# Graph convolution on one core: later program places for the stores of gathered rows, 88 early tiles for 92, and a node stage on fixed PSUM banks

## The chip, the cores and the metric

The kernel runs on one core of a Trainium2 chip. The metric is the device time of one execution in microseconds (us), the median of several runs; lower is better. The five engines appear in the profile as PE (TensorE matmul, with PEld its weight loads), DVE (VectorE), ACT (ScalarE), POOL (GpSimd) and SP (SyncE, here only a DMA queue).

## The reference, cut to what matters

There are N = 12500 nodes with 160 values each (64 scalars, 32 vectors of 3) and 400000 edges, sorted by destination.

```python
h = jnp.maximum(_layernorm(x, axis=-1), 0.0)
s0, y0 = x0 @ W_sc0 * a, x0 @ W_l1_0 * a        # x0, x1: the parts of h; a: node_vec1
...                                             # s1, y1: the same of x1, a row for each component
w = jax.nn.silu(edge_length_embedded @ fc_W1) @ fc_W2          # 192 weights for each edge
ys0, ys1 = y0[edge_src], y1[edge_src]                          # the gather
mid = products of w, ys and the 4 values of edge_attr          # 96 + 96*3 = 384 for each edge
z = zeros.at[edge_dst].add(mid)                                # the scatter
x = x + (C_S * s + C_X * (z @ W_l2) * a)
```

(Scales are left out, and the last four lines are put in short.) So each node is normalized and mapped once to y and s, each edge takes the row y of its source, and the products are summed by destination.

## The kernel before, in words

Nodes stand in 98 tiles of 128 rows, edges in 3125 tiles of 128, four edge tiles to a block (782 blocks), twelve to a group.

**The node stage** (the loop over q, L424 to L439) takes two node tiles a step and eight a group, in 49 steps. It is a software pipeline: in iteration q each stage function handles step q minus its lag. `center` (DVE, lag 0) makes mean and variance and one tile's rows; `center_second` (ACT, lag 1) the other tile's; `turn_rows` (TensorE, lag 2) transposes them into a PSUM tile pt; `out_of_psum` (ACT L380, lag 3) copies pt to hT; `map_rows` (TensorE L388, L389, lag 4) multiplies hT with the weights into PSUM tiles po; `leave` (ACT L399, lag 5) copies po, scaled, to ys, and at the end of a group stores eight tiles of y to the DRAM tensor y_d with a DMA on ACT's queue (L401); `add_s` (DVE L407, lag 6) adds the self connection to acc. These y_d stores are called by their group, 0 to 12; the last group has two tiles, the others eight.

**The edge stage** (the loop over b) runs for each block: `load` issues four gathers of y rows on POOL (L509, `yg<-y_d,src_sb`; each takes the 128 rows that one edge tile names), eight blocks ahead, into nine buffers; TensorE makes the edge weights (L519, L535); DVE the products (L458 to L470) and the one-hot matrix sel (L552); TensorE sums by destination (L572). The first gather of y_d needs every y_d store to have landed.

**Early rows.** Every 32nd block, 23 of them (`RB`, capped by the number of blocks), doesn't gather y. Its 4 tiles gather rows of x instead, which are there from the start. `gather_x` (L326, `xr<-in_x,src_sb`) issues these 92 gathers on POOL in the node stage, the first half at q = 4, the second at q = 16, into twelve buffers, and stores each four tiles to a DRAM tensor xr_d with one DMA on SP's queue (L329). In the edge stage `made_load` (L644) brings them back as xm, and the functions `made_...` normalize, transpose and map them on DVE, TensorE and ACT, in steps that `plan` spreads over the blocks before.

**What sets the order.** PE, ACT and DVE run their instructions in the order written (`manual_schedule`). SP and POOL don't: when the program is built, the framework lists their instructions by its own estimate of times, and place in the program is a priority. Each queue then runs its list in order. Every direct DMA, on SP's queue or ACT's, also takes one of eight completion counters in turn, in the order of the common list, and is issued only when the DMA before it on the same counter has landed. So each waits for the one eight places before it in the list, whichever queue that is on.

On SP the program writes, in this order: the loads of x, src and dst; at q = 4 the stores of xr_d number 0 to 10, then 23 small weight loads (L218 to L231), one load of edge attributes (raw, L263) and the first block's eight xe loads (L255); at q = 16 the stores 11 to 22; after the loop the edge stage's loads, with the next eight xe loads first. In the list of before, the y_d store of group 2 stands after the third xr_d store, that of group 3 after six weight loads, that of group 4 after the last weight load, that of group 5 after store 12, that of group 6 after store 21, and that of group 7 after the next xe and raw loads. Groups 8 to 12 follow with no SP DMA between them.

On POOL the node stage also has a `partition_all_reduce` (L139), which turns the destinations' minima around, and a few memsets.

Of the kernel before, what the change touches and what calls it, by code (L numbers as in the profile page):

```python
# [10 lines left out]
F32 = mybir.dt.float32  # L11
# [4 lines left out]
PSUM = bass.MemoryType.PSUM  # L16
DRAM = bass.MemoryType.DRAM

P = 128
M0 = 64  # L20
M1 = 32
D = M0 + 3 * M1
# [8 lines left out]
EG = 8  # L31
GN = 8
HN = 2
RB = 24
RS = 32
LO = D - P
EPS = 1e-5
# [5 lines left out]
def kernel(  # L43
# [19 lines left out]
    nc = tc.nc  # L63
# [19 lines left out]

    nr = max(0, min(RB, (NB - 1) // RS - 1))
    RT = nr * GT
    xr_d = dram.tile([max(nr, 1) * P, GT * D], F32, name="xr_d")
# [193 lines left out]
    def by_tile(ap):  # L280
        n = ap.shape[0]
        return ap.rearrange("(t p) c -> p t c", p=min(P, n))
# [9 lines left out]
    with (  # L292
        tc.tile_pool(name="nr", bufs=1) as nrp,
        tc.tile_pool(name="nrx", bufs=12) as nrx,
        tc.tile_pool(name="ny", bufs=2) as ny,
        tc.tile_pool(name="ns", bufs=3) as ns,
        tc.tile_pool(name="nh", bufs=4) as nh,
        tc.tile_pool(name="nd", bufs=3) as nd,
        tc.tile_pool(name="nd_pt", bufs=2, space=PSUM) as nd_pt,
        tc.tile_pool(name="nd_po", bufs=6, space=PSUM) as nd_po,  # L300
    ):
        yss, mvs, ras, hs, lesses, pts, hTs, poss = ({} for _ in range(8))
        steps = [(g, n, j, min(HN, n - j)) for g, n in groups for j in range(0, n, HN)]

        def load_x(g, n):
            if g + n == NT and N % P:
                nc.gpsimd.memset(acc[:, NT - 1, :], 0.0)
            node_dma(g, n, lambda rows, t, p: nc.sync.dma_start(acc[:p, g + t.start:g + t.stop, :],
                                                                by_tile(x[rows, :])))

        def find_x():

            of = src_sb[:, RS * GT:RS * GT * (nr + 1)].rearrange("p (r c) -> p r c", c=RS * GT)[:, :, 0:GT]
            whole = nrp.tile([P, nr, GT], I32, name="whole")
            nc.vector.tensor_scalar(whole, of, 7, None, ALU.arith_shift_right)
            nc.vector.tensor_copy(hi_f.rearrange("p (r c) -> p r c", c=GT), whole)
            nc.vector.tensor_copy(lo_f.rearrange("p (r c) -> p r c", c=GT), of)
            nc.vector.scalar_tensor_tensor(lo_f, hi_f, -float(P), lo_f, op0=ALU.mult, op1=ALU.add)

        def gather_x(lo, hi):  # L320

            for r in range(lo, hi):
                xr = nrx.tile([P, GT, D], F32, name="xr")
                for k in range(GT):
                    c = (r + 1) * RS * GT + k
                    nc.gpsimd.indirect_dma_start(  # L326
                        out=xr[:, k, :], out_offset=None, in_=x,
                        in_offset=bass.IndirectOffsetOnAxis(ap=src_sb[:, c:c + 1], axis=0))
                nc.sync.dma_start(xr_d[r * P:(r + 1) * P, :], xr.rearrange("p t c -> p (t c)"))  # L329

        def center(q):

            g, n, j, m = steps[q]
            xt = acc[:, g:g + n, :]
            if j == 0:
                mvs[g] = ns.tile([P, GN, 2], F32, name="mv")
            mv = mvs[g]
            h = nh.tile([P, HN, D], F32, name="h")
            for k in range(m):
                st = ns.tile([P, 6], F32, name="st")  # L340
                nc.vector.bn_stats(st, xt[:, j + k, :])
                nc.vector.bn_aggr(mv[:, j + k, :], st)
                if k == 0:
                    nc.vector.tensor_scalar(h[:, k, :], xt[:, j + k, :], mv[:, j + k, 0:1], 0.0, ALU.subtract, ALU.max)
                else:
                    less = ns.tile([P, 1], F32, name="less")
                    nc.vector.tensor_scalar(less, mv[:, j + k, 0:1], -1.0, None, ALU.mult)
                    lesses[q] = less
            hs[q] = h
            if j + m == n:  # L350
                ra = ns.tile([P, GN], F32, name="ra")
                nc.scalar.activation(ra[:, :n], mv[:, :n, 1], AF.Sqrt, bias=eps)
                ras[g] = ra

        def center_second(q):

            g, n, j, m = steps[q]
            if m > 1:
                nc.scalar.activation(hs[q][:, 1, :], acc[:, g + j + 1, :], AF.Relu, bias=lesses.pop(q))

        def scales(q):

            g, n, j, m = steps[q]
            if j + m == n:
                ra = ras[g]
                nc.vector.reciprocal(ra[:, :n], ra[:, :n])
                nc.vector.tensor_mul(ra[:, :n], ra[:, :n], a_sb[:, g:g + n])

        def turn_rows(q):
            m, h = steps[q][3], hs.pop(q)  # L370
            pt = nd_pt.tile([P, 2, HN, P], F32, name="pt")
            for k in range(m):
                nc.tensor.transpose(pt[:, 0, k, :], h[:, k, 0:P], ident)
                nc.tensor.transpose(pt[:, 1, k, :], h[:, k, LO:D], ident)
            pts[q] = pt

        def out_of_psum(q):
            m, pt = steps[q][3], pts.pop(q)
            hT = nd.tile([P, 2, HN, P], F32, name="hT")
            nc.scalar.activation(hT[:, :, :m, :], pt[:, :, :m, :], AF.Copy)  # L380
            hTs[q] = hT

        def map_rows(q):
            m, hT = steps[q][3], hTs.pop(q)
            poss[q] = []
            for k in range(m):
                po = nd_po.tile([P, 2, D], F32, name="po")
                nc.tensor.matmul(po[:, :, 0:M0], hT[:, 0, k, :], wn0, start=True, stop=True)  # L388
                nc.tensor.matmul(po[:, :, M0:], hT[:, 1, k, :], wn1, start=True, stop=True)  # L389
                poss[q].append(po)  # L390

        def leave(q):

            g, n, j, m = steps[q]
            if j == 0:
                yss[g] = ny.tile([P, GN, 2, D], F32, name="ys")
            ys, ra = yss[g], ras[g]
            for k, po in enumerate(poss.pop(q)):
                nc.scalar.activation(ys[:, j + k, :, :], po, AF.Copy, scale=ra[:, j + k:j + k + 1])  # L399
            if j + m == n:  # L400
                node_dma(g, n, lambda rows, t, p: nc.scalar.dma_start(by_tile(y_d[rows, :]), ys[:p, t, 0, :]))  # L401

        def add_s(q):

            g, n, j, m = steps[q]
            if j + m == n:
                nc.vector.tensor_add(acc[:, g:g + n, :], acc[:, g:g + n, :], yss[g][:, :n, 1, :])  # L407


        with tc.manual_schedule(engines=engines):  # L410
            load_x(0, HN)
            nc.sync.dma_start(a_sb, attr)
            node_weights()
            load_x(HN, min(GN, NT) - HN) if NT > HN else None
            nc.sync.dma_start(src_sb, src)
            for k, (g, n) in enumerate(groups[1:]):
                load_x(g, n)
                if k == 4:
                    nc.sync.dma_start(dst_i, dst)
            if len(groups) <= 5:  # L420
                nc.sync.dma_start(dst_i, dst)
            last = len(steps) - 1
            half = nr // 2
            for q in range(len(steps) + 6):  # L424
                if q == min(4, last):
                    if RT:
                        find_x()
                        gather_x(0, half)
                    edge_weight_loads()
                    e4_load(0)  # L430
                    load_xe(0)
                if q == min(16, last):
                    first_nodes()
                    if RT:
                        gather_x(half, nr)
                for stage, lag in ((scales, 1), (center_second, 1), (leave, 5), (out_of_psum, 3), (turn_rows, 2), (map_rows, 4),
                                   (center, 0), (add_s, 6)):
                    if 0 <= q - lag <= last:
                        stage(q - lag)  # L439
    with tc.manual_schedule(engines=engines):  # L440
        edge_weights()
    before.close()
# [31 lines left out]
    with (  # L474
# [258 lines left out]
        with order:  # L733
# [17 lines left out]
            for b in range(K * (NG - 1) + 12):  # L751
                g, k = divmod(b, K)
# [3 lines left out]
                if b < NB:  # L756
                    q, r = divmod(b, EG * K)
# [36 lines left out]
    with (  # L794
# [11 lines left out]
        with tc.For_i(0, n, 1) as _:  # L806
# [60 lines left out]
            with tc.For_i(0, NT, 1) as i:  # L867
                zt = fp.tile([P, ZC], F32, name="f_zt")
                nc.sync.dma_start(zt, z_d[ds(i * P, P), :])
                pt = fpp.tile([P, 3, P], F32, name="f_pt")  # L870
# [4 lines left out]
                po = fpp.tile([P, D], F32, name="f_po")  # L875
# [50 lines left out]
```

## Time and profile before

| | us |
|---|---|
| median of 3 runs | 4006.47 (4003.85 to 4008.27) |
| the profiled execution | 4014.25 |
| its span | 4012.4 |
| PE busy | 3864.0 (96%) |
| DVE busy | 3519.4 (88%) |
| ACT busy | 2027.8 (51%) |
| POOL busy | 2979.7 (74%) |

The busy shares are means over both stages. A row of a timeline gives start, duration (both in us), engine, line, operation, tiles, count, and in brackets the idle time of the engine just before and what ended it. A row of the stretches gives for PE, PEld, DVE, ACT and POOL the busy time and the number of instructions, then the granted TensorE clock, the DMA share and GB/s. A row of the waits gives the total, the number of times and the longest. A row of the groups gives busy time, mean ns of one, and the idle time before. SPq and ACTq are the DMA issues of these queues; they are not counted as busy.

### The profile page before, as it was taken

The page shows a single profiled execution, that of the slowest core. Times are in us where ns is not written, and L with a number is a line of the kernel's source. Part 1 is how long each engine was busy: PE and PEld are TensorE (multiplying, and loading weights), DVE is VectorE, ACT ScalarE, POOL GpSimd, SP SyncE. Part 2 cuts the span into 40 slices and gives each one's busy share as a digit, 9 for nine tenths or more (in the row PEclk, how much of TensorE's full clock was granted, in tenths as well). Part 3 has the DMA queues.
Part 4 walks back from the last instruction along what each step waited for, and adds up shares of the span by engine and source line. Part 5 has one row for each costly group of instructions (what it writes and reads, how often), then busy time and mean ns, then how long its engine had stood idle before and what let it go on. Part 6 is the DMA issues. An engine that isn't in the chain of part 4 may idle for free.

```text
span 4012.4 us, 60400 instructions
## 1 busy us (share of the span) xinstructions
PE 3864.0 (96%) x18093; PEld 2382.8 (59%) x18093; DVE 3519.4 (88%) x7697; ACT 2027.8 (51%) x6160; POOL 2979.7 (74%) x3137
## 2 busy tenths in 40 slices
PE   5599999999999999999999999999999999999998
PEld 4455666665666656665666656656566566666655
DVE  6589899898899898898998998998998989989987
ACT  5455555555455544555454554555545554445444
POOL 6477777777777777777777777777777777777775
PEclk8799999999999999999999999999999999999999
DMA  8423333333233233232333323332332323342323
GB/s 254 119 74 79 74 79 77 76 76 78 75 78 79 73 79 77 74 79 73 80 77 76 78 76 76 77 79 73 79 79 74 78 74 79 77 126 75 74 74 83
DMA packets 239795, 334.86 MB, mean 83 GB/s; under 512 B 66506, under 2 KB 183318, under 8 KB 239206
## 3 DMA queue, kind: packets, MB, share of 16 engines
q0 software_dynamic: 150000, 256.20, 25.7%
q1 hardware_dynamic: 75666, 66.32, 5.6%
q10 hardware_dynamic: 13796, 8.44, 0.8%
q8 instruction: 144, 2.36, 0.2%
q14 instruction: 189, 1.55, 0.1%
HBM read 307.16 MB, written 23.54 MB: 82 GB/s over the span
## 4 chain that ended last, share of the span: by engine, by line
PE 69%; DVE 11%; POOL 7%; issue 5%; DMA 5%; ACT 1%; DVEq 1%; SPq 0%; ACTq 0%; POOLq 0%
PE pz L572 40%; PE pw L535 12%; PE px L519 8%; POOL yg L509 5%; DMA yg<-y_d,src_sb 5%; PE px L604 3%; DVE sel L552 3%; PE px L600 3%; POOL xr L326 2%; DVE tmp L460 2%; DVE tmp L458 2%; PE px L586 2%; DVE both L464 1%; DVE pr L470 1%; DVE pr L469 1%
## 5 line engine op out<-in xcount | busy, mean ns | idle before, releaser
L509 POOL DMA_INDIRECT yg<-y_d,src_sb x3033 | 2881.6, 950 | 966.7 <-issue 738.3
L572 PE MATMUL pz<-pr,sel 128*128 128x384 f32 x6250 | 2236.4, 501 | 22.4 <-DVE sel L552 22.3
L572 PEld LDWEIGHTS pz<-pr,sel 128*128 128x128 f32 x6250 | 1128.3, 190 | 827.6 <-issue 152.0
L453 ACT ACTIVATE yge<-yg,raw 128x160 f32<-128x160 f32 x3033 | 1133.0, 428 | 552.5 <-DMA yg<-y_d,src_sb 548.7
L536 ACT ACTIVATE pw<-raw 128x12 f32<-128x12 f32 x782 | 141.9, 181 | 1309.0 <-issue 664.9
L535 PE MATMUL pw<-w,hT 64*128 64x192 f32 x6250 | 722.3, 350 | 26.3 <-DVE pr L470 24.2
L466 DVE TENSOR_TENSOR pr<-both,pw 128x768 f32<-128x768 f32 x782 | 737.7, 943 | 0.0
L458 DVE TENSOR_TENSOR tmp<-yg,pw 128x384 f32<-128x384 f32 x759 | 417.5, 550 | 347.4 <-DMA yg<-y_d,src_sb 275.8
L535 PEld LDWEIGHTS pw<-w,hT 64*128 64x128 f32 x6250 | 491.5, 186 | 334.6 <-issue 92.3
L460 DVE TENSOR_REDUCE tmp<-tmp 128x128 f32<-128x384 f32 x782 | 464.4, 594 | 26.9
L552 DVE TENSOR_TENSOR sel<-pz,drel 128x1536 f32<-128x1536 f32 (+1 forms) x261 | 455.1, 1744 | 0.0
L519 PE MATMUL px<-xe,w 32*128 32x512 f32 x782 | 438.9, 643 | 4.9 <-issue 4.3
L470 DVE TENSOR_TENSOR pr<-pw,yge 128x384 f32<-128x384 f32 x782 | 427.6, 547 | 0.0
L469 DVE TENSOR_TENSOR pr<-pw,yge 128x256 f32<-128x256 f32 x782 | 326.3, 417 | 1.7 <-ACT yge L453 1.7
L464 DVE TENSOR_TENSOR both<-pw,yg 128x256 f32<-128x256 f32 x759 | 314.2, 414 | 0.0
L524 ACT ACTIVATE hT<-px 128x512 f32<-128x512 f32 x391 | 232.7, 595 | 3.0 <-PE px L519 2.8
L465 DVE TENSOR_TENSOR pr<-pw,tmp 128x128 f32<-128x128 f32 x782 | 219.3, 280 | 0.0
L600 PEld LDWEIGHTS px<-os,place 128*128 128x128 f32 x1044 | 169.8, 190 | 69.9 <-ACT ps L615 0.8
L604 PE MATMUL px<-wc,za 128*128 128x96 f32 (+1 forms) x1566 | 210.0, 270 | 0.0
L630 DVE SCALAR_TENSOR_TENSOR acc<-ps,a_sb,acc 128x160 f32 x522 | 198.8, 381 | 11.8 <-ACT ps L615 2.3
L604 PEld LDWEIGHTS px<-wc,za 128*128 128x128 f32 x1566 | 201.7, 191 | 0.5 <-ACT za L590 0.3
L600 PE MATMUL px<-os,place 128*128 128x160 f32 x1044 | 184.7, 299 | 1.1 <-ACT os L610 0.6
(119 smaller groups left out, 2238.8 us busy)
## 6 DMA issues: line engine op xcount, KB each, us to landing
yg<-y_d,src_sb POOLq DMA_INDIRECT x3033
xe<-in_e SPq DMA_DIRECT2D x784, 32.0 KB
y_d<-ys ACTq DMA_DIRECT2D x12, 640.0 KB
xr_d<-xr SPq DMA_DIRECT2D x23, 320.0 KB
xm<-xr_d SPq DMA_DIRECT2D x23, 320.0 KB
acc<-in_x SPq DMA_DIRECT2D x11, 640.0 KB
out<-acc SPq DMA_DIRECT2D x11, 640.0 KB
raw<-in_e SPq DMA_DIRECT2D x32, 192.0 KB
```

The costliest lines, as they stand in the source:

```text
L453: nc.scalar.activation(yge[:, k, :], yg[:, k, :], AF.Copy, scale=e4v[:, k, 0:1])
L458: nc.vector.tensor_tensor(tmp[:, :n, 0:3, :], y1, wt[:, :n, NW:NW + 3].unsqueeze(3).to_broadcast([P, n, 3, M1]), ALU.mult)
L460: nc.vector.tensor_reduce(tmp[:, :n, 3, :], tmp[:, :n, 0:3, :].rearrange("p t c u -> p t u c"), AX.X, ALU.add)
L466: nc.vector.tensor_mul(pr[:, :n, 192:ZC].rearrange("p t (c u) -> p t c u", c=3), both[:, :n, :].unsqueeze(2).to_broadcast([P, n, 3, M0]), ...
L470: nc.vector.tensor_mul(pr[:, :n, 96:192].rearrange("p t (c u) -> p t c u", c=3), wt[:, :n, M0:96].unsqueeze(2).to_broadcast([P, n, 3, M1]) ...
L509: nc.gpsimd.indirect_dma_start(out=yg[:, k, :], out_offset=None, in_=y_d, in_offset=bass.IndirectOffsetOnAxis(ap=src_sb[:, t:t + 1], axis=0))
L519: nc.tensor.matmul(ph, w1[r, :], xe[r, :], start=True, stop=True)
L535: nc.tensor.matmul(pw[:, k, 0:NW], hT[r, o:o + P], w2[r, :], start=True, stop=True)
L552: nc.vector.tensor_tensor(sels[g][:, 0:n, :], pzs[g % 2][:, ZC:].unsqueeze(1).to_broadcast([P, n, WN]), drel[:, g * TG:g * TG + n].unsquee ...
L572: nc.tensor.matmul(z_ps[g], sels[g][:, t % TG, :], pr[:, k, :], start=t % TG == 0, stop=last)
L600: nc.tensor.matmul(px[:, 1 + h, :], place[:, h, :], os[:, :], start=True, stop=True)
L604: nc.tensor.matmul(px[:, 0, lo:hi], za[:, k, :], wc[:, k, lo:hi], start=k == 0, stop=k == 1)
```

## The change

Four things change.

1. `RB` goes from 24 to 22. With 782 blocks it was capped at 23, so 22 blocks and 88 tiles are early now, in place of 23 and 92. The 23rd block gathers y like the rest.
2. `gather_x` no longer stores. The stores go to `keep_x`, which the loop over q calls at its end for store r as soon as 5q is at least 14r + 60 (r = 0 at q = 12, then every 2.8 steps); stores 16 to 21 follow after the loop.
3. The PSUM tiles of the node stage are eight fixed banks, two for pt and six for po, in place of tiles from two pools of the same sizes.
4. In each iteration `out_of_psum` comes before `leave`, the lag of `leave` is 6 (it was 5) and that of `add_s` 7 (it was 6), and the loop has one iteration more. ACT's wait for pt in one iteration so covers the po tiles that it reads next.

```diff
-RB = 24
+RB = 22
...
-        tc.tile_pool(name="nd_pt", bufs=2, space=PSUM) as nd_pt,
-        tc.tile_pool(name="nd_po", bufs=6, space=PSUM) as nd_po,
+        tc.tile_pool(name="nd_banks", bufs=1, space=PSUM) as nd_banks,
     ):
+        pt_banks = [nd_banks.tile([P, 2, HN, P], F32, name=f"pt{i}") for i in range(2)]
+        po_banks = [nd_banks.tile([P, 512], F32, name=f"po{i}") for i in range(6)]
...
+        xrs, kept = {}, [0]
...
-                nc.sync.dma_start(xr_d[r * P:(r + 1) * P, :], xr.rearrange("p t c -> p (t c)"))
+                xrs[r] = xr
+
+        def keep_x(r):
+            nc.sync.dma_start(xr_d[r * P:(r + 1) * P, :], xrs.pop(r).rearrange("p t c -> p (t c)"))
...
-            pt = nd_pt.tile([P, 2, HN, P], F32, name="pt")
+            pt = pt_banks[q % 2]
...
-                po = nd_po.tile([P, 2, D], F32, name="po")
+                po = po_banks[(q * HN + k) % 6][:, 0:2 * D].rearrange("p (v c) -> p v c", v=2)
...
-            for q in range(len(steps) + 6):
+            for q in range(len(steps) + 7):
...
-                for stage, lag in ((scales, 1), (center_second, 1), (leave, 5), (out_of_psum, 3), (turn_rows, 2), (map_rows, 4),
-                                   (center, 0), (add_s, 6)):
+                for stage, lag in ((scales, 1), (center_second, 1), (out_of_psum, 3), (leave, 6), (turn_rows, 2), (map_rows, 4),
+                                   (center, 0), (add_s, 7)):
                     if 0 <= q - lag <= last:
                         stage(q - lag)
+                while kept[0] in xrs and 5 * q >= 14 * kept[0] + 60:
+                    keep_x(kept[0])
+                    kept[0] += 1
+            while kept[0] in xrs:
+                keep_x(kept[0])
+                kept[0] += 1
```

## The prediction

> **What bounds the kernel now.** I read the page's head first, then POOL's waits, then the timeline of each queue in the first 200 us, and the stretches last.
>
> ```profile
> span 4012.4 us, 60400 instructions
> ```
> ```profile
> POOL yg L509 <- issue: 738.3, 2422, 0.3
> POOL yg L509 <- ACT yge L453: 46.9, 154, 0.3
> ...
> POOL yg L509 <- DMA y_d<-ys: 42.4, 1, 42.4
> ```
> ```profile
> 183.23 0.95 POOL L509 DMA_INDIRECT yg<-y_d,src_sb  x1 [42.40 <-DMA y_d<-ys]
> ...
> 3988.18 0.95 POOL L509 DMA_INDIRECT yg<-y_d,src_sb  x1 [0.31 <-issue]
> ```
> ```profile
> 120.00:140.00 20.00, 0.00 (x0) 0.00 (x0) 0.00 (x0) 0.00 (x0) 15.12 (x17) 0.50 0.46 131
> ...
> 3000.00:3500.00 500.00, 494.87 (x2304) 302.47 (x2303) 451.80 (x974) 256.94 (x785) 378.36 (x400) 1.00 0.30 77
> ```
>
> TensorE is busy 494.87 of 500 us in the edge stage, and yet it is not what sets the end. The waits of POOL say so: its third figure is the longest single wait, and every one of its waits but one is 0.3 us, the gap between two gathers. POOL is never held back by a full buffer. It issues 3033 gathers without a pause, the first at 183.23 and the last at 3988.18, which makes (3988.18 - 183.23) / 3032 = 1.255 us a gather. After the last one's end (3989.13) come 23.3 us of drain. So
>
> span = T0 + gathers x 1.255 + 23.3, with T0 = 183.23, the end of POOL's one long wait, for the last y_d store.
>
> What sets T0 is the node stage, and in 120 to 140 us nothing runs there but POOL. The rows of ACT's queue say why; the bracket is the idle time before the instruction and what ended it:
>
> ```profile
> 69.95 0.60 ACT L380 ACTIVATE hT<-pt 128x512 f32<-128x512 f32 x1 [12.78 <-DMA xr_d<-xr]
> ...
> 84.83 0.60 ACT L380 ACTIVATE hT<-pt 128x512 f32<-128x512 f32 x1 [7.13 <-DMA w<-in_fc_w]
> ...
> 105.74 0.60 ACT L380 ACTIVATE hT<-pt 128x512 f32<-128x512 f32 x1 [1.84 <-DMA xr_d<-xr]
> ...
> 145.44 0.37 ACTq L401 DMA_DIRECT2D y_d<-ys  x1
> 145.85 0.60 ACT L380 ACTIVATE hT<-pt 128x512 f32<-128x512 f32 x1 [32.12 <-DMA xe<-in_e]
> ...
> 154.79 0.37 ACTq L401 DMA_DIRECT2D y_d<-ys  x1
> 163.12 0.37 ACTq L401 DMA_DIRECT2D y_d<-ys  x1
> 171.44 0.37 ACTq L401 DMA_DIRECT2D y_d<-ys  x1
> ```
> ```profile
> 42.31 31.80 SPq L329 DMA_DIRECT2D xr_d<-xr  x11
> 74.21 3.62 SPq L218 DMA_DIRECT2D w<-in_fc_w  x8
> 92.39 50.44 SPq L329 DMA_DIRECT2D xr_d<-xr  x12
> ```
> ```profile
> 142.51 0.32 SPq L329 DMA_DIRECT2D xr_d<-xr  x1
> 142.87 3.71 SPq L255 DMA_DIRECT2D xe<-in_e  x8
> 182.53 0.82 SPq L644 DMA_DIRECT2D xm<-xr_d  x2
> ```
>
> ACT stops at four y_d stores (groups 3, 4, 6, 7), and each stop ends with a DMA of SP's queue that shares no data with y_d: an xr_d store, a weight load, an xe load. That is the turn of eight counters: such a y_d store waits for the DMA eight places before it, its partner. SP meanwhile sits in its xr_d stores, each behind four gathers. Group 7 is pinned to the second xe load, behind the last xr_d store (142.51), and leaves at 145.44. Unpinned, a group takes 163.12 - 154.79 = 8.33 us. From group 7's store to T0 it is 183.23 - 145.44 = 37.8 us.
>
> **The change part by part.**
>
> *88 tiles in place of 92.* POOL's early gathers:
>
> ```profile
> 10.83 1.30 POOL L326 DMA_INDIRECT xr<-in_x,src_sb  x1 [0.76 <-DMA src_sb<-in_src]
> ...
> 87.86 1.13 POOL L139 PARTITION_ALL_REDUCE negb<-neg  x1 [6.10 <-DVE mv L342]
> 89.18 1.71 POOL L326 DMA_INDIRECT xr<-in_x,src_sb  x1 [0.19 <-issue]
> ...
> 139.87 0.95 POOL L326 DMA_INDIRECT xr<-in_x,src_sb  x1 [0.30 <-issue]
> ```
> ```profile
> L326 POOL DMA_INDIRECT xr<-in_x,src_sb x39 | 40.1, 1027 | 11.8 <-issue 11.8
> ```
>
> The 39 gathers behind the all-reduce take 140.82 - 89.18 = 51.6 us, 1.32 each, 5.3 a store. Four fewer end the stage's gathers at 140.8 - 5.3 = 135.5. In the edge stage the same four tiles come back as gathers of y_d: 4 x 1.255 = +5.0 us on the engine that bounds. What goes from TensorE is hidden under POOL and gives nothing:
>
> ```profile
> L683 PE MATMUL px<-wn,m_t 128*128 128x64 f32 x184 | 40.0, 299 | 0.0
> L684 PE MATMUL px<-wn,m_t 128*128 128x96 f32 x184 | 38.0, 288 | 0.0
> L685 PE MATMUL px<-a_sb,m_t 128*128 128x98 f32 x184 | 35.7, 276 | 0.0
> L672 PE MATMUL px<-ident,m_h 128*128 128x128 f32 x184 | 35.1, 273 | 0.0
> L672 PE MATMUL px<-ident,m_oh 128*128 128x128 f32 x92 | 25.1, 273 | 0.0
> ```
>
> These sum to 173.9 us for 92 tiles, 1.89 a tile; without POOL's cover, four tiles would give back 7.6 us. POOL's waits of 0.3 us say the cover holds, so the term is +5.0.
>
> *The stores' place.* The question is whether a later place in the program makes a later place in the queue. Two rows say no:
>
> ```profile
> 9.44 0.20 POOL L216 MEMSET w<- 128x128 f32 x1
> ```
>
> This memset stands behind the first 44 gathers in the program, and runs ahead of all of them. And at 182.53 SP issues two xm loads at once: the second belongs to b = 29 of the edge loop, yet the xe load of b = 8 isn't issued by then. On SP and POOL an instruction is listed when, by the builder's estimate, its inputs are there; place only decides between two that are both ready. So on SP the new place does one thing: the 23 weight loads, raw and the eight xe loads of the first block now go ahead of all the stores. No store is held until step 12 + 2.8r.
>
> Now the listing. In that of before, one group of steps spans about 17 weight loads, or 9 to 11 stores or xe loads, or 16 to 18 gathers. The x loads end just before group 2's y_d. So weights and first xe take 23/17 + 9/11 = 2.2 groups and end near group 4's y_d, and 22 stores take another 2.2 to 2.4: the last is listed about group 6's or 7's y_d. On the chip a group of steps, 8.33 us, holds 8.33 / 1.32 = 6 gathers, not 16, and store r cannot leave before its gathers end: the listing runs far ahead of them. Groups 3 and 4 come free (their partners are loads and stores of gathers long landed), group 5 nearly so; but group 6 or 7 is still the first y_d behind SP's last store, and its partner is one of the last eight DMAs that SP lists: stores 18 to 21, with the next xe loads among or behind them. The early gain of 12.78 + 7.13 us is waited off again there.
>
> I take store 20 as group 7's partner. The last store left at 142.51 in before; store 20 comes two stores, 2 x 5.3, earlier: 131.9. The landing I take from the second xe load, issued about 142.87 + 3.71/8 = 143.3 and landed by 145.44: 2.1 to 2.5 us. So group 7 leaves at 134.3, and T0 = 134.3 + 37.8 = 172.1, 11.1 us earlier. Bounds: store 19 gives 16.4 earlier, an xe load behind store 21 gives 5.3, store 18 as group 6's partner 121.3 + 2.4 + 8.33 + 37.8 = 169.8, so 13.4.
>
> [...]
>
> *One signal a step, static banks, leave at lag 6.* No row shows a signal's cost. What ACT waits for on TensorE's po is
>
> ```profile
> ACT ys L399 <- PE po L389: 3.1, 8, 0.6
> ```
>
> at most 3.1 us to gain. The extra lag puts each y_d one step later, 8.33 / 4 = 2.1 us to lose. I take 0: a pinned store hides both. The banks are no tighter than before: two for pt, three steps' worth for po, each emptied one iteration ahead of its next use. The hT copy now stands ahead of the y_d store in ACT's order, so TensorE gets one step further while ACT is stuck.
>
> **Sum:** -11.1 + 5.0 = -6.1 us: span 4006.3. The profiled run took 4014.25, 1.85 outside its span; the median of the timed runs, 4006.47, lies 7.8 below that. The same step from the median: **4000.4 us**. About 0.2% (8 us) is what a measurement of this kernel can tell from no change.
>
> **The rivals.**
> *The places hold* (the lists do follow the program). Then no y_d is pinned: 183.2 - (12.78 + 7.13 + 1.84 + 32.12) + 2.1 = 131.4 for the last y_d, POOL's gathers end later, at 135.5, and T0 = 136.8. That is -46.4 + 5.0 = -41.4: 3965. The slope of the new places, 2.8 steps x 2.08 = 5.8 us a store, fits 5.3; the memset and the xm load speak against. 27%.
> [...] 6%.
> *Slower: group 6 pinned to the last store or an xe load behind it.* If the builder lists SP's DMAs faster than I think, group 6 is the first behind them all, and one group more is left: 137.2 + 2.4 + 8.33 + 37.8 = 185.7, and an xe load behind it 187. Then +2.5 to +4 and +5.0: 4014 to 4016. It decides when group 6's partner lands later than 183.2 + 3 - 46.1 = 140; in before group 6 was held 1.84 us by a store of the middle. 7%.
>
> **How the numbers follow.** My forecast, group 6 or 7 pinned to one of the last stores, gets 60%, its own range 3990 to 4010 (16.4 earlier plus 3.1 gained gives 3992; 5.3 earlier plus 2.1 lost, 4008). A third of it lies over 8 us faster. Faster: 0.27 + 0.21 = 0.48; within: 0.39 + 0.06 = 0.45; slower 0.07. The range has to take in the first rival: 3960 to 4011.
>
> **What would show it.** Right: SP's queue has the weights at 42 us and the stores right behind them; ACT has no stop before group 5; a stop of 20 us or more before a y_d of group 5, 6 or 7, ended by xr_d or xe; first yg gather near 172; 3037 gathers, last end 23 us before the span's. Wrong: ACT without stops and the first yg right behind the last xr gather, at 137 (places hold); the same four stops at the same times (counters aren't it); POOL waits over 0.3 us in the edge stage (TensorE bounds after all, and the 5.0 goes); a stop at group 6 ending past 140 (slower).

## The result and the profile after

The kernel after takes **3996.65 us** (median of 12 runs, 3995.57 to 3999.58); the kernel before took 4006.49 us beside it (12 runs, 4003.85 to 4008.27). The ratio is 0.9976, 95% interval 0.9967 to 0.9985: 9.8 us faster. The forecast was 4000.4.

The head of the page after, one of its stretches in the edge stage, and POOL's waits (total, times, longest):

```profile
span 3993.8 us, 60278 instructions
```
```profile
3000.00:3500.00 500.00, 497.22 (x2320) 303.79 (x2321) 452.57 (x973) 254.19 (x793) 378.43 (x400) 1.00 0.31 76
```
```profile
POOL yg L522 <- issue: 744.9, 2445, 0.3
...
POOL yg L522 <- DMA y_d<-ys: 32.1, 1, 32.1
```

TensorE is busier still, 497.22 of 500 us, but POOL's waits in the edge stage are 0.3 us as before, and its one long wait is 32.1 us in place of 42.4. So POOL still bounds. Its timeline: the last x gather, the first y gather, the last one.

```profile
134.64 0.95 POOL L329 DMA_INDIRECT xr<-in_x,src_sb  x1 [0.31 <-issue]
167.71 0.94 POOL L522 DMA_INDIRECT yg<-y_d,src_sb  x1 [32.12 <-DMA y_d<-ys]
...
3969.45 0.95 POOL L522 DMA_INDIRECT yg<-y_d,src_sb  x1 [0.30 <-ACT yge L466]
```

T0, the start of the first y gather, is 167.71 in place of 183.23: 15.5 us earlier. Four more y gathers give 4 x 1.252 = 5.0 back. That leaves 10.5, and 9.8 were measured. (3969.45 - 167.71) / 3036 is 1.2522 us a gather; the profiled execution of before had 1.2549, which made it 8 us slower than the median. Kernels with and without the change show both paces (last section).

Where the 15.5 us come from is in the queues of SP and ACT. SP, with its weights (L218), first xe loads (L255) and xr_d stores (L335):

```profile
40.90 4.39 SPq L218 DMA_DIRECT2D w<-in_fc_w  x8
...
60.16 57.07 SPq L335 DMA_DIRECT2D xr_d<-xr  x18
117.28 0.94 SPq L255 DMA_DIRECT2D xe<-in_e  x2
...
131.87 0.34 SPq L335 DMA_DIRECT2D xr_d<-xr  x1
132.26 0.44 SPq L255 DMA_DIRECT2D xe<-in_e  x1
138.78 0.34 SPq L335 DMA_DIRECT2D xr_d<-xr  x1
```

And ACT, its y_d stores (L408) of groups 5 to 11:

```profile
78.47 0.37 ACTq L408 DMA_DIRECT2D y_d<-ys  x1
...
120.57 0.37 ACTq L408 DMA_DIRECT2D y_d<-ys  x1
120.98 0.43 ACT L366 ACTIVATE h<-acc,less 128x160 f32<-128x160 f32 x1 [34.41 <-DMA xe<-in_e]
...
134.33 0.37 ACTq L408 DMA_DIRECT2D y_d<-ys  x1
134.74 0.43 ACT L366 ACTIVATE h<-acc,less 128x160 f32<-128x160 f32 x1 [6.46 <-DMA xr_d<-xr]
...
142.07 0.37 ACTq L408 DMA_DIRECT2D y_d<-ys  x1
150.13 0.37 ACTq L408 DMA_DIRECT2D y_d<-ys  x1
158.27 0.37 ACTq L408 DMA_DIRECT2D y_d<-ys  x1
163.15 0.37 ACTq L408 DMA_DIRECT2D y_d<-ys  x1
```

Weights and first xe loads now go at 40.90, and 18 stores follow in one block of 57 us. Groups 0 to 5 leave with no stop of 1 us or more at a store. Then group 6 waits 34.41 us for an xe load (117.28) that stands in SP's list behind 18 stores, and group 7 another 6.46 us for store 20 (131.87). The idle time stands in the bracket of the ACT instruction right behind the store. All that was won by then is waited off, except for the 11 us by which group 7 leaves earlier (134.33 for 145.44).

### The profile page after: what moved, and what is told of

The parts are those of the page before. It is cut to its first block, busy times and chain, and to the rows that moved or that the text cites. A ratio compares the mean times of both kernels' runs of the same rounds, so it can differ in the third digit from the quotient of the medians.

```text
span 3993.8 us, 60278 instructions
## 1 busy us (share of the span) xinstructions
PE 3853.6 (96%) x18057; PEld 2374.6 (59%) x18057; DVE 3510.3 (88%) x7668; ACT 2021.6 (51%) x6145; POOL 2971.4 (74%) x3137
## 2 busy tenths in 40 slices
DMA packets 239506, 334.20 MB, mean 84 GB/s; under 512 B 66474, under 2 KB 183286, under 8 KB 238918
## 4 chain that ended last, share of the span: by engine, by line
PE 68%; DVE 13%; POOL 6%; DMA 5%; issue 5%; ACT 1%; DVEq 1%; SPq 0%; ACTq 0%; POOLq 0%
PE pz L585 39%; PE pw L548 12%; PE px L532 7%; POOL yg L522 6%; DMA yg<-y_d,src_sb 5%; PE px L617 3%; DVE sel L565 3%; PE px L613 3%; DVE tmp L473 2%; DVE tmp L471 2%; PE px L599 2%; DVE both L477 1%; DVE pr L483 1%; DVE pr L482 1%; POOL xr L329 1%
## 5 line engine op out<-in xcount | busy, mean ns | idle before, releaser
L549 ACT ACTIVATE pw<-raw 128x12 f32<-128x12 f32 x782 | 141.6, 181 | 1313.1 <-issue 666.3
```

## The experiments

**Theory.** No engine's work fixes when group 7 leaves: ACT is held at a y_d store by the DMA eight places before it in the common list. When group 7 leaves fixes T0. POOL does the rest at one gather per 1.25 us. The counters stand in the traces: the 940 direct DMAs of before are spread over eight of them, 117 or 118 on each (938 in after, 116 to 118 on each), and ahead of a y_d store ACT waits for the counter that the store itself takes. In before that wait of group 7 ended at 145.38, and its counter is that of the second xe load (issued at 143.35, landed by 145.36); the seven DMAs between them in the list, six xe loads and a raw load, have the other seven. In after group 7's is that of store 20 (131.87), and group 6's that of an xe load (117.78). **Rivals**: the late part is POOL's early gathers or ACT's own work, not the counters; TensorE bounds the edge stage; the place of the stores does nothing and the two other edits bring the gain.

**The first series** held four kernels: the loop's condition dropped, the stores held back in the list (below), before with the new node order, before with 88 tiles.

```diff
-                while kept[0] in xrs and 5 * q >= 14 * kept[0] + 60:
+                while kept[0] in xrs:
```

> The changed kernel, but every store of xr_d is called at the end of the iteration in which its gathers are written (q = 4 for stores 0 to 10, q = 16 for 11 to 21) and no longer waits for 5q >= 14r + 60. Theory (the builder's list decides, and place only ranks what is ready): the weights still go first and the list is the same, so T0 = 167.7 us as in the changed kernel, ACT's stops before the y_d stores of groups 6 and 7 stay 34 and 6 us, and the time is 3997 +- 2. Rival (the new places themselves give the gain): without them the stores go out as before, T0 back near 178 to 183 and the time near 4007 to 4011.

> The changed kernel with one more edge for the builder: store r of xr_d is listed behind the hT copy (ACT) of the iteration in which the program calls it, without any wait on the chip. Theory (y_d stores are pinned to SP's late DMAs by the turn of eight counters): no y_d store is pinned any more; ACT has no stop over 3 us; POOL's last xr gather ends near 135 us and becomes what sets T0, 136 to 138; T0 is 30 us below the changed kernel's 167.7, the time 3966 +- 4. Rival (the traffic of the stores, not the counters, slows the node stage, so the same bytes cost the same whenever they go): T0 stays above 160 and the time above 3988.

> The kernel before with the node stage's part of the change alone (fixed PSUM banks, hT copy ahead of leave, leave at lag 6, add_s at lag 7); stores and 92 tiles as before. Theory: the four stops of ACT stay, since SP's list is the same (group 7 leaves at about 145 us); only the stretch behind the last stop is shorter, by the 4.4 us that it was shorter in the changed kernel (33.4 us from group 7's y_d store to T0, against 37.8): T0 177 to 184, time 4000 to 4007. Rival (the signals and the order are the source of the gain): T0 near 168 and the time near 3991.

> The kernel before with RB = 22 alone: 88 early tiles, stores behind their gathers, old node stage. Theory: group 7 stays pinned behind SP's last store, which goes 5.3 us earlier, so T0 is 178 (183.2 - 5.3); four more gathers at 1.252 us in the edge stage give the 5.0 back: 4006 +- 2.5. Rival (TensorE bounds the edge stage): the four more gathers cost nothing and four tiles' TensorE work of 1.89 us goes, so 4006.5 - 5.3 - 7.6 = 3994.

They ran on a chip on which the kernel before took 5337 us in place of 4006, so their times say nothing of the question. T0 came at 221.00 us in the first and 222.74 us in the second, where 167.7 and 136 to 138 were expected. The ratios are 0.9997 (0.9975 to 1.0020), 1.0029 (1.0014 to 1.0045), 1.0011 (0.9991 to 1.0031) and 1.0001 (0.9980 to 1.0023). Two waits of the first kernel there show why, POOL's and ACT's:

```profile
POOL yg L522 <- ACT yge L466: 902.8, 253, 10.4
```
```profile
ACT pw L549 <- issue: 2864.7, 551, 39.2
```

POOL waits up to 10.4 us for buffers that ACT empties, and ahead of one instruction (L549) ACT idles 2865 us in stops of up to 39 us which no semaphore on record explains (666 us and at most 4.0 in after's own trace). In the node stage, too, ACT has stops of 28.41 and 29.84 us in the first kernel and of 29.81 and 28.24 us in the second, at copies to hT and not behind a y_d store. The model "POOL never waits" doesn't hold there, so T0 doesn't set the end. One thing can still be read: SP's order without the condition is that of after (18 stores in a row, then two xe loads). So the condition 5q >= 14r + 60 itself does nothing.

**The stores held back in the list.** The kernel after, with a listing edge from the latest copy to hT to each store: the store is listed behind it, and the edge (`NoSync`) asks for no wait on the chip. (The traces count 60278 instructions in after and 60273 in this kernel.)

```diff
-            nc.sync.dma_start(xr_d[r * P:(r + 1) * P, :], xrs.pop(r).rearrange("p t c -> p (t c)"))
+            d = nc.sync.dma_start(xr_d[r * P:(r + 1) * P, :], xrs.pop(r).rearrange("p t c -> p (t c)"))
+            tc.add_manual_dep(d.ins, at_q[-1].name, mybir.DependencyInfo(
+                mybir.DependencyClass.NoSync, mybir.DependencyReason.DATA), reason="listed behind")
...
-            nc.scalar.activation(hT[:, :, :m, :], pt[:, :, :m, :], AF.Copy)
+            at_q.append(nc.scalar.activation(hT[:, :, :m, :], pt[:, :, :m, :], AF.Copy).ins)
```

> The kernel of e2_held again (store r of xr_d listed behind the hT copy of its iteration). The first series ran where the kernel before takes 5337 us and ACT stands idle up to 30 us with no release in sight, so it tells nothing of this question. Where the kernel before takes about 4006 us: theory (y_d stores are pinned to SP's late DMAs by the turn of counters): ACT without stops over 3 us, T0 136 to 138, set by POOL's xr gathers, time 3966 +- 4. Rival (the stores' traffic, not the counters): T0 above 160, time above 3988.

Measured: **3968.26 us** beside 4007.89, ratio 0.9902 (0.9885 to 0.9918). ACT's y_d stores, from group 5, and POOL at T0:

```profile
78.43 0.37 ACTq L410 DMA_DIRECT2D y_d<-ys  x1
86.51 0.37 ACTq L410 DMA_DIRECT2D y_d<-ys  x1
94.59 0.37 ACTq L410 DMA_DIRECT2D y_d<-ys  x1
...
124.24 0.37 ACTq L410 DMA_DIRECT2D y_d<-ys  x1
125.29 1.43 ACTq L410 DMA_DIRECT2D y_d<-ys  x2
```
```profile
138.09 0.95 POOL L329 DMA_INDIRECT xr<-in_x,src_sb  x1 [0.30 <-issue]
139.34 0.94 POOL L524 DMA_INDIRECT yg<-y_d,src_sb  x1 [0.30 <-issue]
...
3941.88 0.95 POOL L524 DMA_INDIRECT yg<-y_d,src_sb  x1 [0.30 <-issue]
```

Each group follows the one before by 8.1 to 8.3 us, no stop, and the first y gather stands right behind the last x gather, 28.4 us earlier than in after; the time is 28.4 lower too, measured on another chip. (ACT still has two stops over 3 us, 5.76 and 3.24 us, ahead of groups 2 and 3; both wait for DVE.) The engines do the same work in both kernels (PE is busy 3853.6 and 3853.3 us) and the DMAs move the same 334.20 MB. The edit moves the 22 stores in SP's list, and some xe loads go ahead of them by it. So the stops came from the order of the list, and not from the work or the amount of traffic. That the order acts by the turn of eight counters is shown by the next four kernels, where the time at which group 7 leaves was worked out from the list ahead of the run and came within 0.1 to 0.8 us.

**Each edit by itself**, four kernels side by side, on a chip on which the kernel before took 4015.52 us; the slower pace of the gathers there is in the last section. For each I worked out from its list which DMA group 7 waits for.

Before, with fixed banks, new order and lags (the banks' lines are those of the change):

```diff
...
-                for stage, lag in ((scales, 1), (center_second, 1), (leave, 5), (out_of_psum, 3), (turn_rows, 2), (map_rows, 4),
-                                   (center, 0), (add_s, 6)):
+                for stage, lag in ((scales, 1), (center_second, 1), (out_of_psum, 3), (leave, 6), (turn_rows, 2), (map_rows, 4),
+                                   (center, 0), (add_s, 7)):
```

> The kernel before with the fixed banks, the copy to hT ahead of the y_d store and the later lags, nothing else. Its list still pins group 6 to store 18 and group 7 to an xe load behind store 22. Theory (the node order shortens the way from group 7's store to the first y gather from 37.8 to 33.4 us, as the trace of after shows it): group 7 leaves at 145.5, first y gather at 178.9, time 4002. Rival (the 33.4 comes from the earlier stores or from the four gathers less, not from the order): 183, 4006.5.

```profile
145.61 0.43 ACTq L402 DMA_DIRECT2D y_d<-ys  x1
146.09 0.43 ACT L360 ACTIVATE h<-acc,less 128x160 f32<-128x160 f32 x1 [13.91 <-DMA xe<-in_e]
153.43 0.37 ACTq L402 DMA_DIRECT2D y_d<-ys  x1
...
174.50 0.37 ACTq L402 DMA_DIRECT2D y_d<-ys  x1
```
```profile
179.74 0.95 POOL L510 DMA_INDIRECT yg<-y_d,src_sb  x1 [39.00 <-DMA y_d<-ys]
```

Group 7 leaves with the xe load as in before (145.61, 145.44), and T0 comes 34.1 us later, not 37.8. Order, lags and banks together are worth 3.7 us there. ("Still" holds for group 7 alone: group 6 stops 18.1 us for a late xr_d store here, and 1.84 us for one of the middle in before.) The time was 2.9 us under before, ratio 0.9992 (0.9983 to 1.0001). The interval alone doesn't exclude zero; T0 in the trace is 3.5 us earlier.

Before, with 88 tiles:

```diff
-RB = 24
+RB = 22
```

> The kernel before with 88 early tiles in place of 92, nothing else. Its list pins group 7 to an xe load behind store 21. Theory (POOL bounds, so four gathers less ahead of T0 are four more behind it): group 7 leaves at 140.1, first y gather at 177.9, then 5.0 us more of gathers; time 4006. Rival (TensorE bounds the edge stage, and what it does for four early tiles less counts as well, 7.6 us): 3994.

```profile
139.84 0.41 ACTq L401 DMA_DIRECT2D y_d<-ys  x1
148.97 0.37 ACTq L401 DMA_DIRECT2D y_d<-ys  x1
...
172.17 0.37 ACTq L401 DMA_DIRECT2D y_d<-ys  x1
```
```profile
176.81 0.95 POOL L509 DMA_INDIRECT yg<-y_d,src_sb  x1 [41.48 <-DMA y_d<-ys]
```

T0 is 6.4 us earlier, 5.0 go back in the edge stage, and the time is 1.7 us under before, 0.9996 (0.9987 to 1.0005). The rival with TensorE as the bound wanted 12.5 us; the interval allows 5.2 at most.

After, with the stores back in `gather_x`:

```diff
-                xrs[r] = xr
+                nc.sync.dma_start(xr_d[r * P:(r + 1) * P, :], xr.rearrange("p t c -> p (t c)"))
```

> The kernel after with each store back in the gathering function, ahead of the weights in the program. Its list pins group 6 to store 19 and group 7 to an xe load behind store 21. Theory (the place moves only what the counter's turn makes of it): group 7 leaves at 140.2 in place of 134.3, first y gather at 173.6, time 4002.5. Rival (the place does nothing, all comes from the other two edits): 3996.7.

```profile
140.08 0.44 ACTq L408 DMA_DIRECT2D y_d<-ys  x1
```
```profile
173.54 0.95 POOL L522 DMA_INDIRECT yg<-y_d,src_sb  x1 [38.52 <-DMA y_d<-ys]
```

Group 7 leaves at 140.08 (140.2 was expected), T0 is 173.54 (173.6). The time is 3.7 us under before, 0.9990 (0.9981 to 0.9999); the rival wanted 9.8. So the place does bring 5.8 us of T0, though no store leaves when its new place says: the weights and first xe loads go ahead of the stores, the list shifts, and group 7's turn falls on store 20 and not on an xe load behind store 21.

After, with the old order and lags (the edit of the first of these four, turned round):

> The kernel after with the old order and lags of the node stage, banks still fixed. Its list pins group 6 to store 15 and group 7 to the xe load behind store 19, one store earlier than in after. Theory (the order is worth 4.4 us between group 7's store and the first y gather): group 7 leaves at 129.5, 37.8 us from there to the first y gather at 167.3; time 3996, as after. Rival (the order is worth nothing there, 33.4): 162.9, time 3992. The trace tells: a free group takes 8.3 us by the theory, 8.1 by the rival.

```profile
130.34 0.37 ACTq L408 DMA_DIRECT2D y_d<-ys  x1
130.76 0.60 ACT L387 ACTIVATE hT<-pt 128x512 f32<-128x512 f32 x1 [13.80 <-DMA xe<-in_e]
138.52 0.37 ACTq L408 DMA_DIRECT2D y_d<-ys  x1
146.84 0.37 ACTq L408 DMA_DIRECT2D y_d<-ys  x1
```
```profile
166.37 0.95 POOL L522 DMA_INDIRECT yg<-y_d,src_sb  x1 [31.10 <-DMA y_d<-ys]
```

Group 7 leaves 4 us earlier than in after, since its turn falls on a DMA one store earlier, and 2.7 of the 4 us are lost again on the way to T0: 36.0 us for 33.4 (37.8 was expected). So order and lags are worth 2.7 us here, not 4.4. T0 is even 1.3 us earlier than in after, since where the pin falls counts for more. The time, 10.9 us under before (0.9973, 0.9962 to 0.9984), is that of after to about 1 us and can't tell theory from rival. The trace can: a free group takes 146.84 - 138.52 = 8.32 us, and 150.13 - 142.07 = 8.06 in after. The fixed banks are still in this kernel, so the shorter free group of after comes from order and lags, not from the banks.

**The version that beats both, and where its limit is.** The held kernel again, beside 92 (`RB = 24`) and 72 (`RB = 18`) early tiles:

> The kernel after with its stores listed one by one behind the node stage's copies to hT, once more, beside the next two. Theory: ACT never stops at a y_d store, the last pair leaves at 125.3, the first y gather follows the last x gather without a gap, at 139.3; time 0.990 of before, about 38 us under it. Rival (the first gain belonged to that chip): nearer to after, 0.9976.

> The same with 92 early tiles. Theory (POOL runs from its first x gather to its last y gather without a pause, so a tile costs it the same early or late): first y gather 5.0 to 5.3 later, at 144.5, four gathers fewer behind it, time within 0.5 us of the one with 88. Rival (TensorE bounds the edge stage by now, and what it does for four more early tiles counts, 7.6 us): 5 to 8 us slower, with waits of POOL over 0.3 us.

> The same with 72 early tiles, 16 fewer. Theory: POOL's x gathers would end at 119.3, ahead of the last y_d store, so POOL waits for that again: first y gather at 125.3 + 3.5 = 128.8, 10.5 earlier, and 16 x 1.252 = 20.0 more behind it, 9.5 us slower than with 88. Rival (TensorE bounds the edge stage by now): 16 x 1.89 = 30 us of its work go, so as fast or faster than with 88.

Measured, beside 4003.98 for before: 3966.48 (ratio 0.9906, 0.9890 to 0.9921), 3966.98 (0.9905, 0.9890 to 0.9921) and 3978.53 (0.9934, 0.9920 to 0.9948). The first y gather with 92 tiles, then with 72:

```profile
144.92 0.95 POOL L524 DMA_INDIRECT yg<-y_d,src_sb  x1 [0.30 <-issue]
```
```profile
118.03 0.95 POOL L329 DMA_INDIRECT xr<-in_x,src_sb  x1 [0.30 <-issue]
132.61 0.95 POOL L524 DMA_INDIRECT yg<-y_d,src_sb  x1 [13.63 <-DMA y_d<-ys]
```

With 92 tiles T0 is 5.7 us later than with 88 (139.21 there) and four gathers fewer give it back: 0.5 us apart, no measurable difference. With 72 the x gathers end before y_d is there, POOL waits 13.63 us, and it is 12.05 us slower (9.5 expected: T0 came at 132.61, not 128.8, of which 3.0 us are the last y_d stores, issued at 128.29 for 125.3). In the held kernel POOL gathers with one break, 6.5 us ahead of the all-reduce, from its first row of x to its last row of y. What could still shorten it is on POOL, not in the order of the DMAs.

## Why the prediction was right, and where a size was off

| kernel | group 7 waits for | it leaves: worked out, measured | T0: worked out, measured | us against before: worked out, measured |
|---|---|---|---|---|
| before | an xe load behind store 22 | -, 145.44 | -, 183.23 | - |
| after | store 20 | 134.3, 134.33 | 172.1, 167.71 | -6.1, -9.8 |
| before, new order | an xe load behind store 22 | 145.5, 145.61 | 178.9, 179.74 | -4.5, -2.9 |
| before, 88 tiles | an xe load behind store 21 | 140.1, 139.84 | 177.9, 176.81 | -0.5, -1.7 |
| after, old place | an xe load behind store 21 | 140.2, 140.08 | 173.6, 173.54 | -4.0, -3.7 |
| after, old order | an xe load behind store 19 | 129.5, 130.34 | 167.3, 166.37 | -10.5, -10.9 |

(The row of after was worked out before its trace was seen. Of the four below it, those with the new order were worked out with the 33.4 us of that trace. The last column takes the times expected for these four less 4006.5.)

- *What bounds: POOL.* Right. With T0 and the number of gathers alone, the times of all kernels on the chips where before took 4004 to 4016 us come out within about 1.5 us: for after -15.5 + 5.0 = -10.5, measured -9.8.
- *88 tiles: x gathers end at 135.5, +5.0 in the edge stage.* Right: they end at 134.64 + 0.95 = 135.6, and the kernel with 88 tiles alone, whose T0 fell 6.4 us, gained 1.7. The 7.6 us of TensorE's work stayed hidden.
- *The places don't hold; weights, raw and first xe go ahead of all stores; no stop before group 5.* Right, at 40.90 and 60.16. How the builder comes to its order was the author's reading of two rows; the runs show the orders alone, that of after also without the condition on the places (18 stores, then two xe loads). The rival "the places hold" would have had no stop at group 6; there is one of 34.41 us. Its price was nearly right: a list in which the stores do stand later gives 3966 to 3968, for the 3965 worked out. (22 stores at 9 to 11 a group of steps are 2.0 to 2.4 groups, not 2.2 to 2.4; nothing hangs on it.)
- *Group 6 or 7 pinned to one of the last stores, group 7 to store 20, leaving at 134.3.* Right to 0.1 us, and partly by luck: the working led to stores 18 to 21 and the xe loads among and behind them, and store 20 was picked from these. One store earlier or later moves T0 by 5.3 us in that working; behind store 19 group 7 left 4.0 us earlier (130.34). Group 6 was pinned too, to an xe load behind store 17; it did not matter, since group 7 was let go later still.
- *"the same four stops at the same times (counters aren't it)", 6%.* Fallen: moving SP's stores in the list, and nothing on ACT, took all stops at y_d stores away, 34.41 and 6.46 us in after.
- *One signal, banks, lag: "I take 0: a pinned store hides both".* This is the step whose size was off, and nearly all of what the forecast lacked. The pinned store does hide what lies ahead of it: group 5 leaves at 78.47 in after and at 74.77 with the old order and lags, so the later lag costs 3.7 us there, and group 7 is held past 130 in both. But five groups come behind it and are free, and what they gain isn't hidden. The way from group 7's store to T0, in us:

| from, to | before | before, new order | after | after, old order |
|---|---|---|---|---|
| group 7's store, group 8's | 9.35 | 7.82 | 7.74 | 8.18 |
| group 8's, group 10's | 16.65 | 16.20 | 16.20 | 16.64 |
| group 10's, group 11's | 6.56 | 4.87 | 4.88 | 6.57 |
| group 11's, T0 | 5.23 | 5.24 | 4.56 | 4.64 |
| in all | 37.8 | 34.1 | 33.4 | 36.0 |

  *Group 7 to 8.* ACT waits for TensorE's po, 1.6 us in before (145.4 to 154.8) and 0.7 in after with the old order (130.3 to 138.5):

```profile
ACT ys L399 <- PE po L389: 1.6, 4, 0.6
```
```profile
ACT ys L406 <- PE po L396: 0.7, 2, 0.3
```

  With the new order it doesn't wait for po there at all, which fits the prediction's "TensorE gets one step further while ACT is stuck". Why the old order cost more in before than in after isn't settled. Behind the stop of 32.12 us TensorE had a granted clock of 0.50 from 145.90 to 150.10 and of 0.81 from there to 154.80; for the stop of 13.80 us the clock was not shown. The banks differ too, and neither was tried alone.

  *Group 8 to 10.* DVE sets the pace of a free group. Between the stores of groups 8 and 9 its only idle time is one wait for ra from ACT, in before and then in after:

```profile
161.96 0.20 DVE L366 RECIPROCAL ra<-ra 128x8 f32<-128x8 f32 x1 [0.43 <-ACT ra L352]
```
```profile
146.41 0.20 DVE L373 RECIPROCAL ra<-ra 128x8 f32<-128x8 f32 x1 [0.18 <-ACT ra L359]
```

  These 0.25 us less make 8.3 into 8.1.

  *Group 10 to 11.* Group 11's store leaves before at 178.00, 6.56 us behind group 10's:

```profile
178.00 0.37 ACTq L401 DMA_DIRECT2D y_d<-ys  x1
```

  ACT makes four copies to hT between the two, and in after two: the others already stand ahead of group 10's store. This is the largest part behind the first group, 1.7 us.

  I had bounded the edit at 3.1 us by what ACT waits for on po. Of that wait 1.6 us lie behind the pin, and about as much was won there (1.5); the 2.1 us of the other two parts were not in the bound. Whether the order or the lag does it was not tried alone. The last row of the table belongs to another edit: 5.2 us with 92 early tiles, 4.6 with 88. By what, was not found; in the held kernel with 72 it is 5.4 again.
- *The sum.* -6.1 was forecast and -9.8 measured: 3.7 us from that step, 0.7 at the very end, and 0.7 of scatter the other way.

## What to carry to other kernels

Where DMAs of two queues share completion counters in turn, as the 940 direct DMAs of before share eight, a store on one engine's queue can be held by an unrelated transfer on another's, which itself waits for gathers (32.12 us in before, 34.41 in after): look for a bracket in the timeline that names a DMA without data in common, count eight places back in the list, and list slow transfers behind those that must not wait (3968.26 us for 4007.89 here). A gain or a cost that is hidden ahead of a pinned wait is not hidden behind it (37.8 us from group 7's store to T0 became 34.1 with order, lags and banks alone); follow the path from the pin to the end before an edit is costed at nothing. And where one engine issues all gathers without a pause, work moved from late to early on that engine brought nothing here (88 and 92 early tiles were 0.5 us apart); only less idle time did (28.4 us in the held kernel).

## What the runs showed of the hardware that I had not expected

- The pace of a gather differs between executions. Two kernels with 3037 y gathers and no waits, on one chip, before with 88 tiles and after with the old place, from their groups by line:

```profile
L509 POOL DMA_INDIRECT yg<-y_d,src_sb x3037 | 2877.0, 947 | 966.4 <-issue 738.8 <-ACT yge L453 45.7 <-DVE both L464 45.4
```
```profile
L522 POOL DMA_INDIRECT yg<-y_d,src_sb x3037 | 2885.5, 950 | 964.1 <-issue 727.1 <-ACT yge L466 47.0 <-DVE both L477 45.7
```

  947 and 950 ns of work with the same gaps make 8.5 us over the stage, nearly as much as the whole change. The first of the two took 4004.0 us in its profiled run and 4013.2 to 4017.4 in its ten others. What sets the pace was not found. With differences this small, T0 in the trace is the better witness than the time.
- One chip ran the kernel before in 5337 us, at a granted clock of about 0.88 for 0.99. The first two changed kernels there show stops of ACT of 39.2 and 39.9 us at the longest that the profile gives no releaser for, and holding the stores back brought nothing (1.0029). Why was not settled.
